# A graph layer on one core: 62 instead of 58 row tiles, 70 of 128 rows by ScalarE, its addresses from column 64 of a wider table

## The chip, the cores and the metric

The kernel runs on one core of a Trainium2 chip. A core has five engines with an instruction queue each: TensorE (PE), VectorE (DVE), ScalarE (ACT), GpSimd (POOL) and SyncE (SP), and 16 DMA engines that they share. The metric is the device time of one execution in microseconds (us), lower is better. Before the change it is 1966.89 us, the median of 3 runs (1962.34 to 1968.69).

## The reference

A message-passing layer over 6,250 nodes and 206,250 edges, float32, followed by a residual and a layer norm. Cut to what matters:

```python
w_ij = silu(edge_feats @ rad_W1 + rad_b1) @ rad_W2 + rad_b2
w_ij = w_ij + (silu(chi_scalar @ sph_W1 + sph_b1) @ sph_W2 + sph_b2)     # [edges, 8, 16]
q_i = (x @ Wq).reshape(-1, 8, 16)[receivers]
k_j = (x @ Wk).reshape(-1, 8, 16)[senders]
v_j = (x @ Wv)[senders].reshape(-1, 8, 16)
alpha = (q_i * w_ij * k_j).sum(-1) / sqrt(16) * cutoffs[:, None]
out = segment_sum(alpha[..., None] * v_j, receivers) / 16
return layernorm(x + out)
```

The edges are sorted by receiver. So a receiver's q is near at hand for neighbouring edges, while k and v of the senders have to be fetched row by row: 206,250 rows of 1 KB (128 numbers of k and 128 of v).

## The kernel before

**Tiles.** 128 edges make a tile, 4 tiles a quad (512 edges), 4 quads a group: 403 quads in 101 groups. A first stage computes the table `kv_tab` of k and v for all nodes and stores it in HBM; then one loop (lines 827 to 902) goes through the quads, with a position i in the list `order`.

**Fetching k and v.** `gathers` (line 177) has GpSimd issue one indirect DMA for each tile (line 141, called through `gather`): 128 rows of `kv_tab`, picked by a column of `src_i`. It runs up to 14 quads ahead of the loop, in a ring of 16 buffers.

**Row tiles.** For 58 of the quads, `row_quads` (lines 148 and 149, evenly spread over positions 8 to 401), GpSimd fetches three tiles, and the fourth comes another way: `open_tile` (line 194) makes 128 plain DMAs of one row each, 56 by SyncE and 72 by ScalarE (`ROW_ACT`). The address of a row has to stand in a register of the issuing engine. `load` (line 203) fills up to 32 (SyncE) or 24 (ScalarE) registers with one instruction from a table of addresses, `at_i` (the loads at line 204), and `row` (line 209) issues one copy (line 210). So ScalarE has three loads of 24 addresses in a tile and SyncE one of 32 and one of 24. The tables' numbers come from `turn_rows` (line 805): TensorE turns them so that a quad's 128 addresses lie in one partition, and VectorE writes them to `at_i` with two casts (lines 811 and 812).

**Their place in the order.** The order on each queue is the order of the code. `load_rows` (line 230) is called at the end of every loop turn. It opens tiles six positions before their time, counts a copy as 1 and a load as 6, and hands out to SyncE and ScalarE what is due by then, evenly over the loop. For ScalarE it holds two copies back; `copies` (line 848) puts those around the small copy between the two Silu of the next turn.

**One turn of the loop.** TensorE computes the first layers of quad i + 2 (line 566), q at the edges of quad i + 1 (line 585) and the second layer of quad i + 1 (line 618). ScalarE applies Silu to the first layers of quad i + 2 in two halves (line 603), the first of which waits for TensorE's q (the `mark`). VectorE first waits for the rows of quad i + 1 (line 631), multiplies k by q (line 634), and then for quad i multiplies by the edge weights (line 642), sums over a head (line 644, once a quad), multiplies by the cutoffs (line 647) and multiplies v by that (line 659). TensorE sums messages by receiver (line 670). TensorE's first layers of the next quad need the buffers that Silu has read, so whatever stands in ScalarE's queue ahead of a Silu delays TensorE, and through it VectorE.

Of the kernel before, what the change touches and what calls it, by code (L numbers as in the profile page):

```python
# [15 lines left out]
I32 = mybir.dt.int32  # L16
# [5 lines left out]
SP = mybir.EngineType.SP  # L22
ACT = mybir.EngineType.Activation
WAIT = mybir.DependencyInfo(mybir.DependencyClass.Sync, mybir.DependencyReason.DATA)

P = 128
# [13 lines left out]
QUADS = math.ceil(E / EQ)  # L40
# [8 lines left out]
MSGS = 10  # L49
ACTS = 8  # L50
RING = 16
ROW_TILES = 58
ROW_FIRST = 8
ROW_LAST = 401
ROW_LEAD = 6
ROW_ACT = 72
ROW_LOAD = 6
ROW_CARRY = 2
ROW_UNITS = {SP: 32, ACT: 24}
# [14 lines left out]
def gnn_kernel(ctx, tc, x, src, dst, weight, edges, rad_W1, rad_b1, rad_W2, rad_b2,  # L74
# [14 lines left out]
    nc = tc.nc  # L89
# [47 lines left out]
    def quad_of(name, bufs, width=D):  # L137
        return ep.tile([P, QT, width], F32, name=name, bufs=bufs)
# [8 lines left out]
    order = [g * NQ + j for g in range(NG) for j in (0, 2, 1, 3) if g * NQ + j < QUADS]  # L147
    row_at = [ROW_FIRST + (n + 1) * (ROW_LAST - ROW_FIRST) // ROW_TILES for n in range(ROW_TILES)]
    row_quads = {order[i] for i in row_at}
# [13 lines left out]
    def next_rows(engine, n, loads=True):  # L163

        left = rows_left[engine]
        n = min(n, owed[engine])
        while n > 0 and left and (loads or left[0][0] == 1):
            cost, issue = left.pop(0)
            issue()
            n -= cost  # L170
            owed[engine] -= cost
# [22 lines left out]
    def open_tile(k, at_i):  # L194

        q = order[row_at[k]]
        table = kv_tab.bitcast(U8).rearrange("(o n) b -> o (n b)", o=1)
        row_of[q] = quad_of("wide", 3, P)[:, :2, :].rearrange("p t d -> p (t d)")[:, None, :]

        def rows_by(engine, name, a, b):  # L200
            regs = {}

            def load(e, m):
                regs.update(zip(range(e, e + m), nc.values_load_multi_w_load_instructions(  # L204
                    at_i[q % P:q % P + 1, q // P, e:e + m], engines=(name,), min_val=0,
                    max_val=(N - 1) * ROW_BYTES,
                    skip_runtime_bounds_check_because="senders are nodes")[1]))

            def row(p):
                o = engine.dma_start(row_of[q][p:p + 1, 0, :].bitcast(U8),  # L210
                                     table[:, ds(regs.pop(p), ROW_BYTES)])
                tc.no_tile_sem_insts.add(o.ins.name)
                tc.add_to_no_dep_group(f"rows_{q}", o.ins)
                o.then_inc(row_sems[k % ROW_SEMS], 16)
                row_count[k % ROW_SEMS] += 16
                row_done[q] = row_sems[k % ROW_SEMS], row_count[k % ROW_SEMS]
                row_issued[q] = row_issued.get(q, 0) + 1

            items = []
            for e in range(a, b, ROW_UNITS[name]):  # L220
                m = min(ROW_UNITS[name], b - e)
                items.append((ROW_LOAD, lambda e=e, m=m: load(e, m)))
                items += [(1, lambda p=p: row(p)) for p in range(e, e + m)]
            rows_left[name] += items
            return sum(cost for cost, _ in items)

        n = P - ROW_ACT
        row_open.append({SP: rows_by(nc.sync, SP, 0, n), ACT: rows_by(nc.scalar, ACT, n, P)})

    def load_rows(i, at_i):  # L230

        tiles = min(max((i - ROW_FIRST + ROW_LEAD) * ROW_TILES / (ROW_LAST - ROW_FIRST), 0), ROW_TILES)
        while len(row_open) < math.ceil(tiles):
# [5 lines left out]
        next_rows(SP, owed[SP])  # L239
        next_rows(ACT, owed[ACT] - (ROW_CARRY if tiles < ROW_TILES else 0))  # L240

# [106 lines left out]
    with tc.tile_pool(name="nodes", bufs=1) as nodes, \  # L348
# [156 lines left out]
        n = len(chunks)  # L505
# [17 lines left out]
        for i, (k, n) in enumerate(work):  # L523
# [7 lines left out]
            if i >= len(chunks):  # L531
                kv_of[k[0]] = kvs
                a, b = ((j - len(chunks)) * (math.ceil(NT / P) - 1) // XQ for j in (i, i + 1))
# [26 lines left out]
    with tc.tile_pool(name="ps", bufs=1, space=PSUM) as pp, tc.tile_pool(name="loop", bufs=1) as lp:  # L560
# [239 lines left out]
            nc.vector.tensor_scalar(general, found, 0.0, None, op0=OP.is_gt)  # L800

        rows_f = quad_of("kq", 3).rearrange("p t d -> p (t d)")[:, :QUADS]
        at_i = lp.tile([P, math.ceil(QUADS / P), P], I32, name="at_i")

        def turn_rows():
            pt = pp.tile([P, EQ], F32, name="pq", bufs=2).rearrange("p (t d) -> p t d", d=P)
            full = QUADS // P
            for i in range(full + 1):
                n = min(P, QUADS - i * P)
                nc.tensor.transpose(pt[:n, i, :], rows_f[:, i * P:i * P + n], ident)  # L810
            nc.vector.tensor_copy(at_i[:, :full, :], pt[:, :full, :])
            nc.vector.tensor_copy(at_i[:n, full, :], pt[:n, full, :])

        written, ready, ready_at = [], [], []
        load_rel(1, lp, 2)
# [11 lines left out]
        for g in range(NG - 1):  # L827
            for slot, j in enumerate((0, 2, 1, 3)):
                q = g * NQ + j
# [64 lines left out]
                if g == NG - 2 and slot == 0:  # L894
                    n = nc.values_load(general, min_val=0, max_val=1)
# [4 lines left out]
                if i == 0:  # L900
                    turn_rows()
# [242 lines left out]
```

## Time and profile before

| | us |
|---|---|
| median of 3 runs | 1966.89 |
| the profiled execution's own time | 1962.43 |
| its span in the profile | 1960.5 |
| busy: TensorE, VectorE, GpSimd, ScalarE | 1785.3, 1521.0, 1471.3, 644.3 |
| GpSimd: 1522 gathers of k and v, one | 0.946 |
| ScalarE: 806 Silu of 128 x 512, one | 0.689 |
| ScalarE: 4176 row copies issued, 174 address loads | not counted as busy |
| SyncE: 3248 row copies issued, 116 address loads | not counted as busy |

The page counts an engine busy only while it computes. Issuing a DMA and loading registers is work of the engine's sequencer, which the page writes with a q (ACTq, SPq); ScalarE's 33% says nothing on how full its queue is. The chain of waits follows the work that ended last back from the end, each step to what released it. A gather's 0.946 us is GpSimd's work on its descriptors, and the data lands later. Times in the timeline count from the start of the span.

### The profile page before, as it was taken

How to read it: one execution, taken by the hardware profiler on the slowest of the kernel's cores; microseconds unless marked ns; L12 is line 12 of the kernel's file. 1: busy time of each engine (PE TensorE's matmuls, PEld its weight loads, DVE VectorE, ACT ScalarE, POOL GpSimd, SP SyncE). 2: the span in 40 equal slices, each digit the busy share in tenths (PEclk: the TensorE clock that was granted, in tenths of full speed). 3: DMA queues.
4: the chain of work that ended last, by engine and by line, in shares of the span. 5: the costliest groups of instructions: out<-in, count | busy, mean ns of one | idle time of the engine just before them, and what ended most of it. 6: DMA issues, size and time to landing. Idle time of an engine off the chain costs nothing.

```text
span 1960.5 us, 55953 instructions
## 1 busy us (share of the span) xinstructions
PE 1785.3 (91%) x16005; PEld 1498.5 (76%) x16005; DVE 1521.0 (78%) x3366; ACT 644.3 (33%) x1361; POOL 1471.3 (75%) x1562
## 2 busy tenths in 40 slices
PE   9999999998999999888988899989899898988888
PEld 7777777777877777777877777777777777777777
DVE  6787888778887787777777777877777777777778
ACT  3333333332333333333333333333333333323234
POOL 7777777777777777777777777777777777777775
PEclk9999999998999999989989999999899999999999
DMA  9755555555555555555545554555555555545543
GB/s 324 222 144 147 166 145 164 152 145 150 166 144 151 168 145 149 165 143 152 168 142 146 161 155 144 147 168 145 145 150 166 143 145 161 155 142 148 163 133 99
DMA packets 148925, 307.13 MB, mean 157 GB/s; under 512 B 40326, under 2 KB 76608, under 8 KB 148608
## 3 DMA queue, kind: packets, MB, share of 16 engines
q0 software_dynamic: 74080, 201.69, 36.8%
q1 hardware_dynamic: 64400, 96.98, 15.2%
q10 hardware_dynamic: 10128, 4.82, 1.2%
q8 instruction: 127, 2.08, 0.4%
q14 instruction: 190, 1.56, 0.3%
HBM read 289.88 MB, written 15.11 MB: 156 GB/s over the span
## 4 chain that ended last, share of the span: by engine, by line
ACTq 24%; POOL 16%; DMA 16%; DVE 14%; issue 13%; PE 10%; ACT 3%; POOLq 0%; DVEq 0%
ACTq L210 19%; POOL kv L141 16%; DMA kv<-kv_tab,src_i 16%; ACTq L204 5%; PE pw L618 4%; DVE kq L634 3%; DVE side L644 2%; PE pq L585 2%; DVE kq L642 2%; ACT act L603 2%; DVE msg L659 2%; PE ph L566 2%; PE po L670 1%; DVE side L647 1%; PE pq L711 0%
## 5 line engine op out<-in xcount | busy, mean ns | idle before, releaser
L141 POOL DMA_INDIRECT kv<-kv_tab,src_i x1522 | 1439.7, 946 | 465.5 <-issue 395.4
L603 ACT ACTIVATE act<-ph,b 128x512 f32<-128x512 f32 x806 | 554.5, 689 | 1265.6 <-issue 752.0
L618 PE MATMUL pw<-w,act 128*128 128x128 f32 x6448 | 875.0, 292 | 0.0
L618 PEld LDWEIGHTS pw<-w,act 128*128 128x128 f32 x6448 | 796.3, 201 | 52.8 <-issue 7.7
L566 PE MATMUL ph<-feats,w 32*128 32x512 f32 x1612 | 600.0, 665 | 54.3 <-ACT act L603 51.5
L634 DVE TENSOR_TENSOR kq<-pq,kv 128x512 f32<-128x512 f32 (+1 forms) x404 | 270.6, 670 | 358.3 <-DVEq L631 197.3
L585 PE MATMUL pq<-q,hotT 32*128 32x128 f32 x3224 | 490.0, 292 | 5.9 <-DVE kq L634 5.8
L585 PEld LDWEIGHTS pq<-q,hotT 32*128 32x128 f32 x3224 | 408.6, 193 | 26.0 <-DVE kq L634 21.3
L566 PEld LDWEIGHTS ph<-feats,w 32*128 32x128 f32 x1612 | 180.6, 188 | 206.2 <-ACT act L603 149.9
L644 DVE TENSOR_REDUCE side<-kq 128x32 f32<-128x512 f32 x404 | 280.3, 694 | 14.0
L659 DVE TENSOR_TENSOR msg<-kv,side 128x512 f32<-128x512 f32 (+1 forms) x404 | 269.1, 666 | 13.9
L642 DVE TENSOR_TENSOR kq<-pw,kq 128x512 f32<-128x512 f32 x404 | 274.6, 680 | 0.0
L573 PE MATMUL pw<-brow,onesb 3*128 3x512 bf16 x403 | 158.2, 393 | 0.0
L670 PE MATMUL po<-msg,hot 128*32 128x128 f32 x3200 | 153.6, 289 | 0.0
L711 PE MATMUL pq<-part,to 128*128 128x128 f32 x196 | 45.2, 314 | 77.5 <-DVE kq L634 77.5
L670 PEld LDWEIGHTS po<-msg,hot 128*32 128x32 f32 x3200 | 71.1, 110 | 37.9 <-issue 3.8
L711 PEld LDWEIGHTS pq<-part,to 128*128 128x128 f32 x196 | 31.1, 200 | 87.5 <-DVE kq L634 79.2
L647 DVE TENSOR_TENSOR side<-side,scale 128x32 f32<-128x32 f32 x400 | 79.8, 199 | 13.7
L301 DVE TENSOR_TENSOR hotT<-relb,side 128x512 f32<-128x512 bf16 x101 | 68.7, 681 | 1.5 <-DMA relb<-rel_pair 1.5
L306 DVE TENSOR_TENSOR hot<-rel,side 128x512 f32<-128x512 f32 x100 | 68.0, 680 | 0.0
L295 PE MATMUL pq<-wq,xT 128*128 128x128 f32 x200 | 43.0, 298 | 25.9 <-DVE kq L634 25.7
L295 PEld LDWEIGHTS pq<-wq,xT 128*128 128x128 f32 x200 | 31.0, 195 | 31.8 <-DVE kq L634 28.0
(133 smaller groups left out, 824.9 us busy)
## 6 DMA issues: line engine op xcount, KB each, us to landing
wide<-kv_tab ACTq DMA_DIRECT2D x4176, 1.0 KB
wide<-kv_tab SPq DMA_DIRECT2D x3248, 1.0 KB
feats<-in_edges SPq DMA_DIRECT2D x50, 1024.0 KB
kv<-kv_tab,src_i POOLq DMA_INDIRECT x1522, 3.2
relb<-rel_pair SPq DMA_DIRECT2D x50, 256.0 KB
x<-in_x SPq DMA_DIRECT2D x101, 64.0 KB
out<-y SPq DMA_DIRECT2D x101, 64.0 KB
kv_tab<-kv SPq DMA_DIRECT2D x12, 512.0 KB
```

The costliest lines, as they stand in the source:

```text
L141: return nc.gpsimd.indirect_dma_start(out=o, out_offset=None, in_=table, in_offset=bass.IndirectOffsetOnAxis(ap=index, axis=0))
L210: o = engine.dma_start(row_of[q][p:p + 1, 0, :].bitcast(U8), table[:, ds(regs.pop(p), ROW_BYTES)])
L566: return nc.tensor.matmul(act_of[q, i], w1[r0:r0 + R, :], feats_of[g][r0:r0 + R, c0:c0 + EQ], start=True, stop=True)
L573: nc.tensor.matmul(pw, onesb[f:f + 3, :], brow[f:f + 3].rearrange("p t d -> p (t d)"), start=True, stop=False)
L585: o = nc.tensor.matmul(pq_of[q][:, t, :], hotT_of[g][b, t * P:(t + 1) * P], q_of[g][b, :], start=True, stop=True)
L603: o = nc.scalar.activation(act, act_of[q, i], AF.Silu, bias=b1[:, i:i + 1])
L618: o = nc.tensor.matmul(pw[:, t, :], act_of[q, i][:, t * P:(t + 1) * P], w2[:, i, :], start=False, stop=(t == QT - 1 and i == 1))
L634: o = nc.vector.tensor_tensor(kq_of[q][:, u, :], pq_of[q][:, u, :], kv[:, :, :D], op=OP.mult)
L642: nc.vector.tensor_tensor(m, pw_of[q][:, t, :], m, op=OP.mult)
L644: nc.vector.tensor_reduce(alpha, m.rearrange("p t (h e) -> p t h e", e=HD), AX.X, OP.add)
L659: nc.vector.tensor_tensor(msg_of[q][:, u, :].rearrange("p t (h e) -> p t h e", e=HD), kv[:, :, D:].rearrange("p t (h e) -> p t h e", e=HD) ...
L670: o = nc.tensor.matmul(po_of[g][j * W:(j + 1) * W, :], hot_of[g][:, j * QT + t, :], msg_of[g * NQ + j][:, t, :], start=(t == 0), stop=(t = ...
```

## The change

Four numbers change, and with them the table of addresses:

```diff
-ROW_TILES = 58
+ROW_TILES = 62
...
-ROW_ACT = 72
+ROW_ACT = 70
+ROW_AT = {SP: 0, ACT: 64}
...
             def load(e, m):
+                c = ROW_AT[name] + e - a
                 regs.update(zip(range(e, e + m), nc.values_load_multi_w_load_instructions(
-                    at_i[q % P:q % P + 1, q // P, e:e + m], engines=(name,), min_val=0,
+                    at_i[q % P:q % P + 1, q // P, c:c + m], engines=(name,), min_val=0,
...
-        at_i = lp.tile([P, math.ceil(QUADS / P), P], I32, name="at_i")
+        at_i = lp.tile([P, math.ceil(QUADS / P), ROW_AT[ACT] + 80], I32, name="at_i")
...
-            nc.vector.tensor_copy(at_i[:, :full, :], pt[:, :full, :])
-            nc.vector.tensor_copy(at_i[:n, full, :], pt[:n, full, :])
+            m = P - ROW_ACT
+            for a, b, at in ((0, m, ROW_AT[SP]), (m, P, ROW_AT[ACT])):
+                nc.vector.tensor_copy(at_i[:, :full, at:at + b - a], pt[:, :full, a:b])
+                nc.vector.tensor_copy(at_i[:n, full, at:at + b - a], pt[:n, full, a:b])
```

62 quads now have a row tile, each of 58 copies by SyncE (loads of 32 and 26 addresses) and 70 by ScalarE (loads of 24, 24 and 22). ScalarE's addresses began at column 56 of 128 and begin at column 64 of 144. In the changed program lines from 194 on stand two lower, those of `turn_rows` up to four.

On GpSimd the whole loop is one run of gathers. Before, around it (`iota` ahead, and the load of the verdict `general` behind):

```order
L337 IOTA col 128x128
L339 IOTA row 128x1
L141 DMA msg<-in_x,src_x 128x128 x32
L141 DMA kv<-kv_tab,src_i 128x256 x1522
L895 TENSOR_LOAD general
```

and now:

```order
L339 IOTA col 128x128
L341 IOTA row 128x1
L142 DMA msg<-in_x,src_x 128x128 x32
L142 DMA kv<-kv_tab,src_i 128x256 x1518
L899 TENSOR_LOAD general
```

Four gathers are gone, nothing else moved there.

On ScalarE, the middle of the loop, from the first Silu of one quad to the first Silu two quads on (`act` is a Silu's output, `xT` and `tot` small copies, `wide` a row copy's target, `at_i` the addresses). Before:

```order
L603 ACTIVATE act_102<-ph,b_72 128x512
L210 DMA wide<-kv_tab 1x1024
L290 ACTIVATE xT<-pq 128x128
L210 DMA wide<-kv_tab 1x1024
L603 ACTIVATE act_103<-ph,b_72 128x512
L210 DMA wide<-kv_tab 1x1024 x11
L603 ACTIVATE act_104<-ph,b_72 128x512
L210 DMA wide<-kv_tab 1x1024
L715 ACTIVATE tot<-pq 128x128
L210 DMA wide<-kv_tab 1x1024
L603 ACTIVATE act_105<-ph,b_72 128x512
L210 DMA wide<-kv_tab 1x1024 x3
```

The last line goes on with a load and three more copies ahead of the next Silu. The same place now:

```order
L605 ACTIVATE act_102<-ph,b_72 128x512
L212 DMA wide<-kv_tab 1x1024
L292 ACTIVATE xT<-pq 128x128
L212 DMA wide<-kv_tab 1x1024
L605 ACTIVATE act_103<-ph,b_72 128x512
L212 DMA wide<-kv_tab 1x1024 x12
L605 ACTIVATE act_104<-ph,b_72 128x512
L212 DMA wide<-kv_tab 1x1024
L717 ACTIVATE tot<-pq 128x128
L212 DMA wide<-kv_tab 1x1024
L605 ACTIVATE act_105<-ph,b_72 128x512
L212 DMA wide<-kv_tab 1x1024 x6
```

Behind the last line now only a load stands ahead of the next Silu. The first quad has 14 copies instead of 13, the second 8 and a load as before.

## The prediction

> **What bounds the kernel now.** The page comes first: no engine is full by its busy time, and the chain of work that ended last is split over several, ScalarE's issuing sequencer (ACTq) ahead.
>
> ```profile
> PE 1785.3 (91%) x16005; PEld 1498.5 (76%) x16005; DVE 1521.0 (78%) x3366; ACT 644.3 (33%) x1361; POOL 1471.3 (75%) x1562
> ACTq 24%; POOL 16%; DMA 16%; DVE 14%; issue 13%; PE 10%; ACT 3%; POOLq 0%; DVEq 0%
> ```
>
> Such an average hides two stages. The same chain asked for by stretches shows them, here 244 to 705.6 us and then 900 to 1900 us:
>
> ```profile
> by line: ACTq L210 47.5%; issue 14.8%; ACTq L204 12.1%; ACT act L603 5.7%; PE pw L618 3.5%; PE pq L585 2.0%; PE ph L566 1.9%; DVE kq L634 1.7%; DVE side L644 1.5%; DVE kq L642 1.3%; PE po L670 0.9%; ACT y L746 0.8%; DVE msg L659 0.6%; DVE s
> ```
>
> ```profile
> by line: DMA kv<-kv_tab,src_i 27.5%; POOL kv L141 27.4%; issue 12.2%; DVE kq L634 4.7%; DVE side L644 3.6%; PE pw L618 3.2%; DVE kq L642 3.1%; DVE msg L659 2.6%; PE pq L585 2.3%; ACTq L210 2.1%; PE ph L566 1.6%; PE po L670 1.2%; DVE side L6
> ```
>
> Early, ScalarE's row copies (L210) and address loads (L204) set the pace; later GpSimd's gathers and their landing do. The waits of VectorE for those gathers (its wait L631) say the same: absent from the first stretch, whose longest is quoted, 196.7 us in the rest.
>
> ```profile
> DVE kq L634 <- PE pq L585: 70.1, 71, 2.4
> ```
>
> ```profile
> DVE kq L634 <- DVEq L631: 196.7, 130, 4.2
> ```
>
> Next, the pace of each side. One reduction L644 runs per quad, so its counts by stretch are quads:
>
> ```profile
> 244.00:705.60 461.60, 69.53 (x100) 0.97 0.53 153
> 705.60:1912.20 1206.60, 175.16 (x252) 0.94 0.53 152
> ```
>
> The early pace is 461.6 / 100 = 4.616 us a quad, the later one 1206.6 / 252 = 4.788. GpSimd's own pace never changes:
>
> ```profile
> L141 POOL DMA_INDIRECT kv<-kv_tab,src_i x1522: 942/946/1221, 44.4 to 1947.2; - x191
> ```
>
> ```profile
> 1899.72 0.94 POOL L141 DMA_INDIRECT kv<-kv_tab,src_i  x1 [0.30 <-issue]
> ...
> 1947.23 0.95 POOL L141 DMA_INDIRECT kv<-kv_tab,src_i  x1 [0.30 <-issue]
> ```
>
> Those two are 38 gathers apart: 47.51 / 38 = 1.2503 us each; and (1947.2 - 44.4) / 1521 = 1.251 over the whole run, so GpSimd never stops. A row tile lets one quad in 393 / 58 do with three gathers, so its pace in the loop is 1.2503 x (4 - 58 / 393) = 4.816 us a quad. ScalarE's side at 4.616 is quicker, eats the lead that GpSimd has at the start, and then waits for it. **The kernel is GpSimd-bound, with ScalarE close behind**: at its early pace ScalarE's side would reach the quad of 1912.2 us (352 quads on from 244) at 244 + 352 x 4.616 = 1868.8, which is 43.4 us of slack.
>
> **Part 1, GpSimd.** Four row tiles more are four gathers fewer: -4 x 1.2503 = **-5.0 us** at the end of its string, if nothing else becomes later. That is all the gain there is.
>
> **Part 2, ScalarE.** Its copies go from 58 x 72 = 4176 to 62 x 70 = 4340 (+164), its address loads from 174 to 186. The timeline of ScalarE shows what one costs:
>
> ```profile
> 222.56 0.69 ACT L603 ACTIVATE act<-ph,b 128x512 f32<-128x512 f32 x1 [3.76 <-issue]
> 222.70 0.47 ACTq L210 DMA_DIRECT2D wide<-kv_tab  x1
> ...
> 223.25 0.23 ACTq L210 DMA_DIRECT2D wide<-kv_tab  x1
> ...
> 223.57 2.93 ACTq L210 DMA_DIRECT2D wide<-kv_tab  x9
> 226.55 0.69 ACT L603 ACTIVATE act<-ph,b 128x512 f32<-128x512 f32 x1 [2.56 <-issue]
> 226.62 0.58 ACTq L210 DMA_DIRECT2D wide<-kv_tab  x2
> ...
> 227.32 3.40 ACTq L210 DMA_DIRECT2D wide<-kv_tab  x11
> 230.78 0.69 ACT L603 ACTIVATE act<-ph,b 128x512 f32<-128x512 f32 x1 [2.79 <-issue]
> ...
> 232.74 2.38 ACTq L210 DMA_DIRECT2D wide<-kv_tab  x7
> 235.16 0.69 ACT L603 ACTIVATE act<-ph,b 128x512 f32<-128x512 f32 x1 [2.96 <-issue]
> ```
>
> ```profile
> L204 ACTq TENSOR_LOAD <-at_i x174: 1669/1809/2004, 77.6 to 1918.6; - x174
> ```
>
> From Silu to Silu the quads take 3.99 us with 11 copies, 4.23 with 13, and 4.38 with 7 copies and a load. Eleven copies in a string take 3.40 us: (3.40 - 0.23) / 10 = 0.317 each. The two copies under the first Silu are there in either kernel, so each added one stands in such a string: 164 x 0.317 = 52.0 us (the pair of 11 and 13 would make it 0.12, the whole pace less 0.45 loads of 1.81 over 10.6 copies at most 0.36). Loads: 12 x 1.81 = 21.7. The third load of a tile has 22 addresses, not 24. No 22 is in the trace; two loads of SyncE, the first with 32 and the second with 24, give the slope:
>
> ```profile
> L204 SPq TENSOR_LOAD <-at_i x1: 2263/2263/2263, 371.3 to 371.3; - x1
> ```
>
> ```profile
> L204 SPq TENSOR_LOAD <-at_i x1: 1724/1724/1724, 389.5 to 389.5; - x1
> ```
>
> (2.263 - 1.724) / 8 = 0.067 an address, so 62 x 2 x 0.067 = -8.4 (none to this much). In all 52.0 + 21.7 - 8.4 = **+65.3 us of ScalarE's queue** over 393 quads, 0.166 a quad. The Trainium skill ("Runtime: NRT & Kernel Launch", Instruction fetch mechanics) puts a register's load at about 200 ns even in bulk; an estimate by that page would be 164 x 0.2 = 32.8 instead of 13.3 for the loads, 84.8 us in all instead of 65.3. The trace's 0.067 speaks against it and decides.
>
> Does ScalarE's side feel all of that? Its waits in the early stretch:
>
> ```profile
> ACT act L603 <- issue: 256.3, 83, 4.4
> ACT act L603 <- PE pq L585: 48.5, 17, 5.5
> ```
>
> In 17 of 100 quads TensorE released the Silu, and a longer string there may be free. So between 0.83 x 0.166 = 0.138 and 0.166 a quad; with d for it, the quad of 1912.2 is reached at 244 + 35d (about 35 quads with rows before 244) + 352 x (4.616 + d) = 1868.8 + 387d. **The point of balance is d = 0.112**, and GpSimd's -5.0 is had only under 0.099. With 0.138 it is 1922.2, +10.0; with 0.166 1933.0, +20.8. I take the middle, **+15 us**. ScalarE then bounds the whole run, 4.616 + 0.152 = 4.768 against GpSimd's new 1.2503 x (4 - 62 / 393) = 4.804: quicker by so little that the lead of the start is never used up.
>
> Is it given back behind 1912? No: VectorE there goes without pause to the last gather's quad.
>
> ```profile
> 1910.97 0.69 DVE L634 TENSOR_TENSOR kq<-pq,kv 128x512 f32<-128x512 f32 x1 [0.96 <-DVEq L631]
> ...
> 1915.57 0.55 DVE L634 TENSOR_TENSOR kq<-pq,kv 128x384 f32<-128x384 f32 x1
> ...
> 1947.24 0.56 DVE L634 TENSOR_TENSOR kq<-pq,kv 128x384 f32<-128x384 f32 x1 [0.63 <-DVEq L631]
> ```
>
> **Part 3, the edits at nothing.** SyncE gets 62 x 58 = 3596 copies for 3248, 8 loads more, and 26 addresses for 24 in the second: 348 x 0.317 + 8 x 1.99 (the mean of the two loads quoted) + 62 x 2 x 0.067 = 135 us of its queue. What hides them is its waiting for TensorE:
>
> ```profile
> SPq L324 <- PE pq L585: 218.4, 73, 10.1
> SPq L256 <- PE pq L585: 113.9, 45, 4.6
> ```
>
> 332 us cover 135; without that cover SyncE's rows come late (rival 2). The table's two casts become four:
>
> ```profile
> L811 DVE CAST at_i<-pq x1: 550/550/550, 70.3 to 70.3; 128x384 int32<-128x384 f32 x1
> L812 DVE CAST at_i<-pq x1: 267/267/267, 70.7 to 70.7; 19x128 int32<-19x128 f32 x1
> ```
>
> Between the same 0.8 us and twice it; they end near 71 and ScalarE's first load starts at 77.6, so nothing is taken; without that cover up to +0.8. Starting ScalarE's addresses at column 64 is taken at nothing too: its loads start at columns 56, 80 and 104 now, SyncE's quoted 24 at column 32, 1.72 against 1.81. That difference may lie in the engine or the column.
>
> **Rivals.**
>
> 1. *Not slower: ScalarE absorbs its copies and GpSimd stays the bound.* For it: the 196.7 us that VectorE waits late in the run, and the 43.4 of slack. It decides under d = 0.099, which copies at 0.12 give ((19.7 + 21.7 - 8.4) / 393 = 0.084). Then -5.0. Against it: the string of eleven at 0.317. The Trainium skill ("Perfetto Trace Analysis", DMA Optimizations) advises balancing DMAs over the engines that issue them where issuing binds; by that rule this would be the outcome, but the early chain shows ScalarE's queue binding as well. Between this and the forecast lies a near balance, 0 to +5.
> 2. *SyncE's rows come late.* If its waits stand between the copies and cannot be shifted, a row tile lands after its quad and VectorE's wait L631 stays. It decides once more than 332 of waiting less 135 is lost; 0.5 us in each of 62 tiles is +31.
> 3. *Column 64 makes loads quicker.* One load a tile at 1.72: 62 x 0.09 = 5.6 us, d less by 0.014, +9.5 instead of +15.
> 4. *A copy costs its upper end*, 0.36: d = 0.184 or more, +28 to +36.
>
> **How the numbers follow.** The profiled execution took 1962.43 us (span 1960.5), the fastest of those shown but one; the median of before is 1966.89, 4.5 above it. Forecast 1962.4 + 15 = 1977.4 for a like execution, **1982** beside the median. Chances: forecast, with rival 3, 0.57; rival 4 0.08; rival 2 0.04; near balance 0.11; rival 1 0.20. About 0.3% (5.9 us) is what a measurement of this kernel can tell from no change. Rival 1's -5.0 is 0.25%, so it is halved between faster and same: faster 0.10, same 0.10 + 0.11 = 0.21, slower 0.69. The range goes from 1960, two under rival 1's 1961.9, to 2000, near the upper end of the copies' price.
>
> **What would show it.** Right: VectorE's waits at L631 shrink from 196.7 us to under 60, GpSimd's last gather still starts 5 us earlier (near 1942), ScalarE's copies and loads lead the chain of the late stretch too, and L644 counts about 4.77 us a quad throughout. Wrong: the late chain still led by gathers (rival 1), or L631 waits on row tiles while the gathers have landed (rival 2), or ScalarE's loads under 1.75 us (rival 3).

## The result, and the profile after

The changed kernel takes 2029.24 us (4 runs, 2028.77 to 2029.70) against 1967.07 before: 1.0313 times as long, 95% interval 1.0300 to 1.0327, 62 us more. 1982 was forecast, 1960 to 2000 the range. Slower, as forecast, and by four times as much.

The runs e5 to e16 were made on three other chips, where the granted TensorE clock was about 0.85 instead of 0.95 and the kernel before itself took 2502 to 2534 us, so their times are compared with that alone.

The page's first line and the chain that ended last, on the changed kernel:

```profile
PE 1848.1 (91%) x16005; PEld 1523.1 (75%) x16005; DVE 1522.7 (75%) x3376; ACT 644.6 (32%) x1361; POOL 1468.9 (72%) x1558
ACTq 61%; issue 14%; PE 10%; ACT 7%; DVE 3%; DVEq 0%
```

GpSimd's 16% and its gathers' 16% are gone from the chain, and ScalarE's queue holds 61% instead of 24%. Here is the stretch from 900 to 1900 us, where gathers led before:

```profile
by line: ACTq L212 50.6%; issue 14.7%; ACTq L206 13.4%; ACT act L605 5.6%; PE pw L620 4.3%; PE ph L568 2.9%; PE pq L587 2.3%; DVE kq L636 0.8%; DVE kq L644 0.7%; DVE side L646 0.7%; PE po L672 0.5%; ACT y L748 0.5%; ACT q L299 0.4%; ACT tot
```

L212 are ScalarE's row copies and L206 its address loads. VectorE's waits from 705.6 to 1980 us no longer name its wait for rows (L633 now, L631 before, when it was 196.7 us for the gathers), only TensorE, which waits for Silu:

```profile
DVE kq L636 <- PE pq L587: 272.2, 212, 4.4
DVE kq L636 <- issue: 9.1, 7, 3.2
```

GpSimd has its lead and is held back by the `mark`, which lets no gather run ahead of TensorE. Before, no wait of a gather for TensorE was longer than the usual pause of 0.3 us; now 25.4 us are put to it, of which 37 x 0.3 are that pause. Its last gather starts at 1957.0, 15 us behind the 1942 forecast:

```profile
POOL kv L142 <- PE pq L587: 25.4, 37, 2.6
```

```profile
1957.00 0.95 POOL L142 DMA_INDIRECT kv<-kv_tab,src_i  x1 [0.30 <-issue]
```

The reductions of the late stretch, one a quad:

```profile
705.60:1912.20 1206.60, 171.69 (x247) 0.96 0.53 150
```

1206.6 / 247 = 4.885 us a quad (one reduction more or less in the stretch is 0.02). ScalarE's side ran at 4.616 early in the kernel before, so it is 0.27 slower, where 0.152 was forecast. What it does from Silu to Silu shows where:

```profile
256.54 0.69 ACT L605 ACTIVATE act<-ph,b 128x512 f32<-128x512 f32 x1 [3.54 <-issue]
256.62 0.61 ACTq L212 DMA_DIRECT2D wide<-kv_tab  x2
...
257.34 4.08 ACTq L212 DMA_DIRECT2D wide<-kv_tab  x12
261.47 0.69 ACT L605 ACTIVATE act<-ph,b 128x512 f32<-128x512 f32 x1 [3.50 <-issue]
261.54 0.58 ACTq L212 DMA_DIRECT2D wide<-kv_tab  x2
...
264.16 2.39 ACTq L212 DMA_DIRECT2D wide<-kv_tab  x6
266.60 0.69 ACT L605 ACTIVATE act<-ph,b 128x512 f32<-128x512 f32 x1 [3.70 <-issue]
```

A quad of 14 copies takes 4.93 us, one of 8 and a load 5.13. Of the twelve copies in the string, four take 0.31 to 0.32 instead of 0.228, so they start 0.342 apart, where the eleven of the prediction took 0.317. These two strings overstate the change: over all strings of ten or more copies the mean distance is 0.328 before and 0.338 now. And the loads changed; first all of them by engine, then one of ScalarE's of 22 addresses, at 282.8 us:

```profile
L206 ACTq TENSOR_LOAD <-at_i x186: 1672/1845/2201, 79.8 to 1986.5; - x186
L206 SPq TENSOR_LOAD <-at_i x124: 2067/2184/2457, 75.6 to 1969.8; - x124
```

```profile
L206 ACTq TENSOR_LOAD <-at_i x1: 2047/2047/2047, 282.8 to 282.8; - x1
```

Before, no load of ScalarE passed 2004 ns, and SyncE's shortest took 1673. Fewer addresses (22 for 24) take longer (a mean of 2.03 us against 1.81), and SyncE's 26 take as long as its 32 (2.18 and 2.20).

### The profile page after: what moved, and what is told of

Its sections match the earlier page's. It is cut to its first block, busy times and chain, and to the rows that moved or that the text cites. A ratio compares the mean times of both kernels' runs of the same rounds, so it can differ in the third digit from the quotient of the medians.

```text
span 2026.9 us, 57021 instructions
## 1 busy us (share of the span) xinstructions
PE 1848.1 (91%) x16005; PEld 1523.1 (75%) x16005; DVE 1522.7 (75%) x3376; ACT 644.6 (32%) x1361; POOL 1468.9 (72%) x1558
## 4 chain that ended last, share of the span: by engine, by line
ACTq 61%; issue 14%; PE 10%; ACT 7%; DVE 3%; DVEq 0%
ACTq L212 48%; ACTq L206 13%; ACT act L605 5%; PE pw L620 4%; PE ph L568 2%; PE pq L587 2%; DVE kq L636 1%; DVE side L646 1%; DVE kq L644 1%; PE po L672 1%; ACT y L748 0%; ACT q L299 0%; ACT tot L717 0%; ACT part L708 0%; ACT xT L292 0%
## 5 line engine op out<-in xcount | busy, mean ns | idle before, releaser
L620 PE MATMUL pw<-w,act 128*128 128x128 f32 x6448 | 889.8, 295 | 0.0
L620 PEld LDWEIGHTS pw<-w,act 128*128 128x128 f32 x6448 | 809.7, 204 | 51.7 <-issue 5.5
L568 PE MATMUL ph<-feats,w 32*128 32x512 f32 x1612 | 689.2, 656 | 156.3 <-ACT act L605 151.9
L568 PEld LDWEIGHTS ph<-feats,w 32*128 32x128 f32 x1612 | 212.6, 188 | 378.6 <-ACT act L605 350.0
L587 PE MATMUL pq<-q,hotT 32*128 32x128 f32 x3224 | 478.5, 288 | 0.0
L587 PEld LDWEIGHTS pq<-q,hotT 32*128 32x128 f32 x3224 | 400.7, 191 | 1.1 <-issue 1.0
L748 ACT ACTIVATE y<-y,shift,rs 128x128 f32<-128x128 f32 x98 | 48.7, 497 | 0.0
L394 PE MATMUL pk<-wkv,xT 128*128 128x256 f32 x162 | 39.1, 381 | 3.1 <-DVE kv L396 3.1
```

The source lines that it names most:

```text
L568: return nc.tensor.matmul(act_of[q, i], w1[r0:r0 + R, :], feats_of[g][r0:r0 + R, c0:c0 + EQ], start=True, stop=True)
L587: o = nc.tensor.matmul(pq_of[q][:, t, :], hotT_of[g][b, t * P:(t + 1) * P], q_of[g][b, :], start=True, stop=True)
L620: o = nc.tensor.matmul(pw[:, t, :], act_of[q, i][:, t * P:(t + 1) * P], w2[:, i, :], start=False, stop=(t == QT - 1 and i == 1))
```

## The experiments

Theories. **Count**: copies and loads at the forecast's prices, only more of them. **Length**: a load whose addresses don't come out even costs more. **Collision**: the two queues delay each other's copies, so that more of SyncE's make ScalarE's slower.

The sums in this table are worked out from each trace by adding the durations of all instructions of a kind. The pace is 1206.6 us divided by the reductions counted in the stretch from 705.6 to 1912.2. The time is the median of the runs, the trace that of one of them: 1962.4 us before, 2028.8 changed, 1996.7 in e4, 1998.9 in e18. The 4.788 of before and e3 is set by GpSimd; that of e4 and e18 by ScalarE, whose queue has 60 and 59% of their chains.

| kernel | copies ScalarE / SyncE | ScalarE's copies, us | its loads, us | us a quad | time, us |
|---|---|---|---|---|---|
| before | 4176 / 3248 | 1014.2 | 314.6 | 4.788 | 1967 |
| changed | 4340 / 3596 | 1087.9 | 350.8 | 4.885 | 2029.2 |
| e1 | 4464 / 3472 | 1096.4 | 334.9 | 4.885 | 2025.7 |
| e2 | 4340 / 3596 | 1099.0 | 336.3 | 4.885 | 2018.8 |
| e3 | 4060 / 3364 | 999.9 | 326.6 | 4.788 | 1969.2 |
| e4 | 4340 / 62 | 1047.8 | 348.5 | 4.788 | 1986.0 |
| e17 | 4216 / 3720 | 1080.5 | 321.1 | 4.885 | 2010.8 |
| e18 | 4340 / 2046 | 1053.6 | 349.8 | 4.788 | 2008.1 |

**e1: the number of tiles alone.**

```diff
-ROW_TILES = 58
+ROW_TILES = 62
```

> 62 row tiles, nothing else changed: 72 copies a tile by ScalarE, loads of 24 and 32 addresses only, the old table. ScalarE has 4464 copies and 186 loads. Theory 'count' (a copy 0.317 us, a load 1.81 and the slow first copy behind it): (288 x 0.317 + 12 x 2.1) / 393 = 0.30 us a quad more than 4.616, so 4.91 a quad and about 2033 us. Theory 'length' (a load whose number of addresses is no multiple of 8 costs more, which made the changed kernel slower than forecast): none here, so the same 2033, and its loads stay at 1.81 and 2.18. Theory 'collision' (more copies on SyncE's queue make each of ScalarE's slower): ScalarE's copies last some 8 ns more as in the changed kernel, 5.0 a quad and about 2060 us.

2025.71 us, 1.0298 of before (1.0281 to 1.0315). Its loads keep their price:

```profile
L204 ACTq TENSOR_LOAD <-at_i x186: 1683/1805/2047, 75.2 to 1980.1; - x186
```

Count and length gave 2033, collision 2060: plain counting is near. Four tiles more slow the kernel with the old split and table too, and shifting two copies of a tile to SyncE, as the change does, gained nothing against it.

**e2: every load at full length.** Each load of the changed kernel takes 24 or 32 addresses, and the table is filled so far.

```diff
-                    at_i[q % P:q % P + 1, q // P, c:c + m], engines=(name,), min_val=0,
+                    at_i[q % P:q % P + 1, q // P, c:c + ROW_UNITS[name]], engines=(name,), min_val=0,
```

> The changed kernel, but every load takes a full 24 (ScalarE) or 32 (SyncE) addresses; the last ones are loaded and not used. 'length': ScalarE's third load falls from 2.03 to 1.81, 62 x 0.22 = 14 us less than the changed kernel, about 2015 us; if the length also causes the slower copies, down to the forecast's 1983. 'collision': ScalarE's copies stay at a mean of 0.250 us, and the time at 2015 or above. 'count': 2015.

2018.76 us, 1.0267 (1.0251 to 1.0284), some 10 us under the changed kernel, 14 expected. Here are its loads:

```profile
L206 ACTq TENSOR_LOAD <-at_i x186: 1670/1808/2029, 75.2 to 1976.1; - x186
```

Loading 24 and using 22 is cheaper than loading 22. ScalarE's copies stay slow (a mean of 1099.0 / 4340 = 0.253 us), so the length doesn't cause that.

**e3: the split and the table without the tiles.** The changed kernel with `ROW_TILES = 58`.

> The changed kernel with 58 row tiles: 70 copies a tile by ScalarE, 4060 in all, loads of 24, 24, 22 and 32, 26. 'count': less work for ScalarE than before, early pace 4.616 - 116 x 0.317 / 393 = 4.52 us a quad, GpSimd stays the bound, 1967 us. 'length': third loads at 2.03 add 58 x 0.22 / 393 = 0.03, 4.55 early, still 1967. 'collision': SyncE's 3364 copies instead of 3248 add about 0.03 more, 4.58, still 1967. Above 1975 would speak for something in the table or the split that none of them names.

1969.20 us, 1.0009 (0.9992 to 1.0027): no change, by all three. VectorE waits for gathers at L633 as before the change:

```profile
DVE kq L636 <- DVEq L633: 208.5, 140, 5.2
```

So ScalarE still has slack there, and its longer loads cost nothing. It is the four tiles that turn the bound over.

**e4: SyncE's copies taken away.** ScalarE's queue is that of the changed kernel. SyncE brings 58 neighbouring rows with one DMA, so that the choice of those rows is left out, and with its copies go its loads.

```diff
+            if name == SP:
+                rows_left[name] += [(1, rows)]
+                return 1
...
+                o = engine.dma_start(row_of[q][a:b, 0, :], kv_tab[a:b, :])
```

> The changed kernel, but SyncE brings its 58 rows of a row tile with one DMA of neighbouring rows of the table instead of 58 copies (so it leaves the choice of rows out for them) and has no address loads. ScalarE's queue is untouched. 'collision': ScalarE's copies fall to 0.228 to 0.233 us behind the first of a load, some 12 to 20 ns each or 50 to 80 us over 4340, about 1960 to 1985. 'length' and 'count': ScalarE's queue takes as long as in the changed kernel, 2029 us, third loads still 2.03.

1985.96 us, 1.0109 (1.0080 to 1.0137): 43 us less than the changed kernel, 1 us over the upper end of what collision gave. The profiled execution was the slowest of its four, 32 us under the changed kernel's. Its reductions in the late stretch, 1206.6 / 252 = 4.788 a quad, and the chain that ended last, which ScalarE's queue still leads:

```profile
705.60:1912.20 1206.60, 175.12 (x252) 0.95 0.51 151
ACTq 60%; issue 15%; PE 12%; ACT 8%; DVE 3%; DMA 1%; SPq 0%; DVEq 0%
```

The same 4340 copies of ScalarE lasted 1087.9 - 1047.8 = 40 us less in all. **The collision is shown**: ScalarE's copies take longer because SyncE fetches its rows one by one beside them. Few of them get slower: the median is 0.228 us in both kernels, and of the copies that don't stand behind a load, 258 took more than 0.3 us in the changed kernel and 61 here (79 in the kernel before). Whether it is SyncE's issuing, the many small transfers that follow from it, or its loads with them, this run doesn't tell, as it takes away all three; e15 below, which keeps the loads, has no usual footing.

**e17: 68 copies by ScalarE, 60 by SyncE**, loads of 24, 24, 20 and 32, 28 addresses.

```diff
-ROW_ACT = 70
+ROW_ACT = 68
```

> 62 row tiles, 68 copies by ScalarE (loads of 24, 24 and 20) and 60 by SyncE (32 and 28), once more, for a chip on which the kernel before takes 1967 us. 'Count': GpSimd binds, 1962 us. 'Collision': ScalarE's copies delayed by 40 us or more in all, 0.10 to 0.16 us a quad over 4.616, 1965 to 1985 us.

2010.79 us, 1.0234 (1.0216 to 1.0252), above everything expected. Two things are new in its trace. The chain that ended last has the landing of row copies and SyncE's queue in it, and VectorE waits at L633 again, this time for row copies:

```profile
ACTq 51%; issue 13%; PE 12%; DMA 8%; ACT 6%; DVE 6%; SPq 3%; DVEq 0%
ACTq L212 41%; ACTq L206 10%; DMA wide<-kv_tab 8%; ACT act L605 5%; PE pw L620 4%; SPq L212 3%; PE ph L568 3%; PE pq L587 2%; DVE kq L636 1%; PE pk L394 1%; DVE kq L644 1%; DVE side L646 1%; PE po L672 1%; PE pt L384 0%; ACT y L748 0%
```

```profile
DVE kq L636 <- DVEq L633: 70.5, 18, 10.6
```

And SyncE has no time left. Of its waits for TensorE, 332 us before, 130.9 + 80.6 are left in the changed kernel and 2.3 here (first the changed kernel's, then e17's):

```profile
SPq L326 <- PE pq L587: 130.9, 67, 5.3
SPq L258 <- PE pq L587: 80.6, 43, 4.9
```

```profile
SPq L258 <- PE pq L587: 2.3, 5, 1.0
```

That is rival 2, at 60 copies a tile instead of 58. In each split of 62 tiles tried so far, one queue or the other is over.

**e18: SyncE with 32 copies and one load a tile**, the other 26 rows by one DMA (their choice left out).

```diff
-            for e in range(a, b, ROW_UNITS[name]):
+            for e in range(a, 32 if name == SP else b, ROW_UNITS[name]):
...
+            if name == SP:
+                items += [(1, lambda: rows(32))]
```

> SyncE with 32 copies and one load of 32 a tile, and one DMA of neighbouring rows for the other 26 (the choice of those left out), for a chip on which the kernel before takes 1967 us; ScalarE's queue is that of the changed kernel. 'Collision by number of SyncE's copies': about 2010 us, ScalarE's copies at a mean of 0.246 us. 'Collision only where both queues are nearly full' (SyncE's idle time fell from about 18 to 12 to 1 us in 100 as its copies went from 3248 to 3596 to 3720, and ScalarE's delays rose with it): close to the 1986 of one DMA, mean 0.242.

2008.11 us, 1.0228 (1.0191 to 1.0264), the value of "by number". But its four runs spread from 1998.9 to 2021.8, and the profiled one is the fastest of them: there ScalarE's copies are nearly as quick as in e4 (a mean of 0.243 and 0.241), and its 1998.9 us lie beside the 1996.7 of e4's profiled execution, which speaks for the other. **Not settled** by the times. The traces lean to the other too: take of each copy of ScalarE that doesn't stand behind a load what it lasts beyond 0.228 us, and the sum is 13.9 us with 62 DMAs of SyncE (e4), 18.3 with 2046 (e18), 19.1 with 3248 (before), 31.2 with 3364 (e3), 32.0 with 3472 (e1), 52.4 and 63.5 with 3596 (changed, e2) and 73.1 with 3720 (e17). It hardly grows up to the kernel before and steeply behind it, where SyncE's waiting for TensorE runs out (332 us there, 212 in the changed kernel, 4 in e17). These kernels differ in more than SyncE's copies, so that is a hint.

**Loads by column: e11.** The changed kernel with ScalarE's addresses from column 58, and so a table 138 wide:

```diff
-ROW_AT = {SP: 0, ACT: 64}
+ROW_AT = {SP: 0, ACT: 58}
```

> Again the changed kernel with ScalarE's addresses from column 58. If only the length counts, the loads stay at 1.81, 1.81 and 2.03 us and the time at 2029. If the start counts, as the run on the other chip has it (3.9 us a load, columns 58, 82 and 106 being no multiples of 4), 186 x 2.0 = 370 us more for ScalarE's queue, 2300 to 2400 us.

2795.37 us in one run, where the kernel before took 2502. Of ScalarE's loads most are three times as long (those up to 2700 us):

```profile
L206 ACTq TENSOR_LOAD <-at_i x181: 289/5092/5725, 108.0 to 2691.8; - x181
```

A partition holds four rows of the table, one behind the other, and with a width of 138 column 58 of the second and fourth starts at a multiple of 4, that of the first and third doesn't. Sorted by where they start, counted so: 24 addresses from a multiple of 4 take 1.75 to 1.81, 24 from any other start 5.44 to 5.49 (76 loads). The start decides far more than the length.

**Loads by length: e12.** The kernel before with `ROW_UNITS = {SP: 30, ACT: 20}`.

> Again the kernel before with loads of 20, 20, 20 and 12 (ScalarE, from columns 56, 76, 96, 116) and of 30 and 26 (SyncE, from columns 0 and 30). If multiples of 4 are cheap in start and length: 20 at 1.53, 12 at 0.98; 30 (28 and 2 left over) at 2.35 to 2.5; the 26 from column 30 far above 2.2, 3 to 5 us. If the number alone counts, that 26 takes 2.18 as in the changed kernel.

2562.46 us in one run, again beside 2502. Some loads here have records far shorter than the rest (down to 13 ns), so medians are given: 1.55 us for 20 addresses and 1.08 for 12. SyncE's 26 from column 30 took 5.57. SyncE's 30 took 2.29, under the 2.35 to 2.5 expected, but longer than the 32 of SyncE in e9 beside the same kernel before (2.11). So a remainder over 4 costs here too, as in ScalarE's 22 and SyncE's 26 of the changed kernel.

**The runs beside a kernel before of 2500 us and more.** Column 58 and the other lengths were each run twice. These were the first runs, with the edits of e11 and e12:

> The changed kernel with ScalarE's addresses beginning at column 58 instead of 64, all lengths as in the changed kernel (24, 24, 22, loaded from columns 58, 82 and 106). If only the length counts, the first two loads stay at 1.81 us and the third at 2.03, and the time at 2029 us. If the start column counts too (58, 82 and 106 are no multiples of 8), the first two take about 2.0, and 62 x 2 x 0.2 = 25 us more, about 2054 us.

> The kernel before with other lengths of load: ScalarE 20, 20, 20 and 12 addresses, SyncE 30 and 26. If a load costs by its number of addresses (0.067 each) 20 takes 1.54 us, 12 1.0, 30 2.13, 26 1.86. If odd lengths cost more, 30 and 26 stand at 2.15 or above, like the 26 of the changed kernel; whether 20 and 12 do, multiples of 4, is open: 1.6 and 1.05 if 4 is the step, above 1.75 if 8 is.

2817.22 and 2596.97 us beside 2529, and the loads read as in e11 and e12. Here are the loads of ScalarE in e7 and then in e8, the long ones and the short:

```profile
L206 ACTq TENSOR_LOAD <-at_i x186: 485/5030/5853, 112.6 to 2774.5; - x186
```

```profile
L204 ACTq TENSOR_LOAD <-at_i x232: 3/1537/1708, 113.0 to 2556.0; - x116
```

The edit of e18, three times:

> As the run with one DMA of SyncE, but SyncE fetches 32 rows of a tile by copies with one load of 32 addresses, and the other 26 with one DMA of neighbouring rows (so it leaves the choice of those rows out). ScalarE's queue is that of the changed kernel. 'collision, by the number of SyncE's copies': 32/58 of the way from 1986 to 2029 us, about 2010, ScalarE's copies at a mean of 0.246 us. 'collision only where SyncE's queue is nearly full' (the delays grew from 17 to 46 us while SyncE's copies grew by 11%): close to 1986, mean 0.242.

> Again SyncE with 32 copies and one load a tile, and one DMA of neighbouring rows for the other 26 (the choice of those left out). 'Collision by number': about 2010 us, ScalarE's copies at a mean of 0.246 us. 'Collision only where SyncE's queue is nearly full': about 1986, mean 0.242.

> SyncE with 32 copies and one load of 32 a tile, and one DMA of neighbouring rows for the other 26 (the choice of those left out). 'Collision by number': about 2010 us, ScalarE's copies at a mean of 0.246 us. 'Collision only where SyncE's queue is nearly full': about 1986, mean 0.242.

0.9933 of the kernel before (0.9914 to 0.9952), 0.9933 (0.9916 to 0.9951) and 0.9939 (0.9922 to 0.9955): 0.6 to 0.7% faster there (with the choice of 26 rows left out), 2.3% slower in e18. The chain of e9 shows why that tells nothing of ScalarE's queue: TensorE holds it, and ScalarE's queue has 6% where it has 61% in the changed kernel on the usual footing.

```profile
PE 58%; issue 15%; DVE 9%; another core or an unknown queue 6%; ACTq 6%; ACT 1%; DVEq 0%
```

The edit of e17, once:

> 62 row tiles, 68 copies by ScalarE (loads of 24, 24 and 20 addresses) and 60 by SyncE (32 and 28): no length with a remainder over 4. ScalarE: 4216 copies, loads 62 x (1.81 + 1.81 + 1.53) = 319 us. 'Count': (40 x 0.317 + 4.7 + 3) / 393 = 0.052 a quad over 4.616, under the balance of 0.112, so GpSimd binds and 1962 us. 'Collision': SyncE's 3720 copies add 40 us or more of delays to ScalarE's, 0.10 to 0.16 a quad, 1965 to 1985 us. 'Length' alone (no collisions): 1962.

1.0255 (1.0238 to 1.0272), near e17's 1.0234, and by the same sign: VectorE waits at L633 for rows of SyncE here too. In this trace, as in those of e5, e9, e14, e15 and e16, most of VectorE's waiting (536 to 794 us) is put to "remote", which the profile doesn't resolve further.

```profile
DVE kq L636 <- DVEq L633: 115.9, 20, 10.4
```

64 copies by each engine, three times:

```diff
-ROW_ACT = 70
+ROW_ACT = 64
...
-ROW_UNITS = {SP: 32, ACT: 24}
+ROW_UNITS = {SP: 32, ACT: 32}
```

> 62 row tiles, 64 copies by each of the two engines, two loads of 32 addresses each: ScalarE 3968 copies and 124 loads of 2.20, SyncE the same. 'count': ScalarE's queue is 208 x 0.317 + (315 - 273) = 108 us shorter than in the kernel before, so it never binds; GpSimd does, 1967 - 5 = 1962 us, if SyncE is in time: its queue grows by 720 x 0.317 + 45 = 273 us against 332 of waiting. 'collision': ScalarE's copies at 0.255 or more take some 50 us back, early pace near 4.5 instead of 4.35, still 1962. If SyncE is late, VectorE waits for row tiles and it is 1975 to 2050.

> Again 62 row tiles, 64 copies by each engine, two loads of 32 addresses each. 'Count': ScalarE's queue is 108 us shorter than in the kernel before and never binds; 1967 - 5 = 1962 us if SyncE is in time. 'Collision': ScalarE's copies at 0.255 or more, early pace 4.5 instead of 4.35, still 1962. If SyncE, whose queue grows by 273 us, is late, VectorE waits for row tiles: 1975 to 2050.

> 62 row tiles, 64 copies by each engine, two loads of 32 addresses each. 'Count': ScalarE's queue is 108 us shorter than in the kernel before and never binds; 1967 - 5 = 1962 us if SyncE is in time. 'Collision': ScalarE's copies at 0.255 or more, early pace 4.5 instead of 4.35, still 1962. If SyncE, whose queue grows by 273 us, is late, VectorE waits for row tiles: 1975 to 2050.

1.0615 (1.0589 to 1.0640), 1.0568 (1.0549 to 1.0587) and 1.0628 (1.0608 to 1.0647): the slowest split of all. The chain of e16 has SyncE's queue ahead, as ScalarE's is in the changed kernel, and VectorE waits for its rows; TensorE has 16%:

```profile
SPq 38%; issue 28%; PE 16%; DVE 8%; another core or an unknown queue 5%; ACTq 3%; DMA 1%; ACT 0%; DVEq 0%
```

```profile
DVE kq L636 <- DVEq L633: 262.9, 37, 11.6
```

So SyncE at 64 copies a tile is over by more than at 60, which goes on from e17. By how much it would be on the usual footing wasn't measured.

SyncE with its loads, and with one copy and one larger DMA behind each in place of the others:

```diff
+                for e in range(a, b, 32):
+                    m = min(32, b - e)
+                    items += [(ROW_LOAD, lambda e=e, m=m: load(e, m)), (1, lambda e=e: row(e)),
+                              (1, lambda e=e, m=m: rows(e + 1, e + m))]
```

> SyncE keeps both address loads of a tile, with 2 copies, and brings the other 56 rows with two DMAs of neighbouring rows (the choice left out). If ScalarE's copies are slowed by SyncE's copies: as with one DMA, 1986 us and a mean of 0.242. If by SyncE's loads: 2029 and 0.250.

1.0148 (1.0131 to 1.0166), the choice of most of SyncE's rows left out. TensorE leads here as well:

```profile
PE 62%; issue 15%; DVE 9%; another core or an unknown queue 6%; ACTq 4%; ACT 1%; DVEq 0%
```

What the loads do to ScalarE's copies can't be read from a run in which ScalarE's queue has slack, so that question stays open. Since the bound is another one there, none of these ratios is carried over.

No version here that fetches the right rows beats the kernel before. GpSimd's whole gain by four tiles is 5 us, and every such split of 62 tiles that was tried on the usual footing makes the kernel at least 45 us slower, by one of the two issuing queues.

## Why the prediction was wrong, point by point

- **What bounds before, and that the bound turns over**: right. The gathers' wait is gone, ScalarE's queue leads the late chain, and e3 beside e1 shows that the tiles do it. The point of balance, 0.112 us a quad, isn't contradicted: e3 lies under it and doesn't move, and e4, e18 and the changed kernel, with 0.17 and 0.27 over 4.616, lie above. Nothing was run close to it.
- **Part 1, GpSimd's -5.0**: no part of it arrives. GpSimd's last gather starts 10 us later than before instead of 5 earlier.
- **Part 2, the +65.3 us of ScalarE's queue, is the step that failed**: that this queue would bind was right, the term about half of what it came to. By the table, its copies last 1087.9 - 1014.2 = 73.7 us more, and 164 x (0.317 - 0.228) = 14.6 us more are estimated to lie between them; its loads last 350.8 - 314.6 = 36.2 more: 124.5 in all, 0.317 a quad. The forecast's factor for what ScalarE feels, 0.83 to 1, agrees: 0.27 / 0.317 = 0.85. Put into the forecast's own formula, 1868.8 + 387 x 0.27 = 1973, 61 us over 1912; in the profiled execution that quad came 66 us later than before, and the medians are 62 apart.
- **Its two mis-sized terms.** Loads: -8.4 for the two addresses fewer was the wrong way round; a load of 22 costs 2.03 instead of 1.81, +13.6, and e2 gets 10 us back. Copies: 52.0 was priced at the spacing that one string of the kernel before showed; it came to 88.3. Of the 36 us between, 3 are the slower first copies behind twelve more loads and 33 are longer copies elsewhere. The price had only the added copies in it: that the copies already there would become slower stood at nothing, without a reason. With SyncE's copies and loads taken away (e4) the same sum for the copies is 1047.8 - 1014.2 + 14.6 = 48.2, close to the 52.0, and the kernel takes 1986, close to the 1982 forecast; some of that nearness is luck, since e4's loads of 22 still cost more than forecast. That SyncE's fuller queue made the difference between the kernel before and this one is inferred from e4 and the row of sums behind e18, not shown apart. The string of eleven at 0.317 was a quiet place as well, against 0.328 in the mean of the long strings.
- **Part 3, SyncE at nothing**: its rows are in time, so rightly nothing by being late; its cover shrank from 332 to 212 us, 120 against the 135 estimated. But this queue, taken as idle enough, is what slows ScalarE's.
- **The rivals.** 1 didn't happen. 2 didn't happen at 58 copies and did in e17 at 60. 3 didn't happen: the full loads of 24 still take 1.81. The start column matters, but 56, 80 and 104 were as good as 64, being multiples of 4; 58 is what column 64 avoids. 4's upper end of 0.36 a copy gave +36 at most, without a term for the copies that were there already; the mean of all rose from 0.243 to 0.251.
- **The tail behind 1912** was not given back, as forecast: from that quad's reduction to the last one it took 42 us before and 42 now.

## What to carry to other kernels

Where an engine issues hundreds of small DMAs between its computing, its busy share says nothing; read the spacing of the copies, and ask what the other issuing queue will do while they go out. A price taken from one queue holds at the load that the other queue had in that trace. When a row count or a split is changed, keep each load of registers a multiple of 4 addresses, from a start that is a multiple of 4, even if some are loaded for nothing: e2 won 10 us by that, and lengths from 12 to 32 are what was seen here.

## What the runs showed of the hardware that was not expected

- In e11 a register load from a start that is no multiple of 4 (32-bit) columns takes 5.47 us for 24 addresses in the mean, 0.228 each, against 1.81 from a multiple of 4. A load of 22 from such a multiple takes 2.03 in the changed kernel, that of 20 a mean of 1.57 in e17: the two left over cost some 0.23 each. The prediction set the 200 ns a register of the Trainium skill ("Runtime: NRT & Kernel Launch", Instruction fetch mechanics) aside for the trace's 0.067; the traces now show both, 0.06 to 0.07 for each address more where loads are even and about that page's figure where they are not. Whether it is the same cost isn't shown.
- The first copy that ScalarE issues behind a load takes 0.475 us instead of 0.228 (mean over each tile's first, 25th and 49th copy, in the kernel before and the changed one), 0.25 us that a load's own duration doesn't show.
- Between the kernel before and the changed one, ScalarE's copies grew by 3.9% and SyncE's by 10.7%, and the time that ScalarE's lasted beyond 0.228 us each grew from 62.1 to 98.4 us. How that comes about on the chip stays open.
